# Decoder attention of a two-layer graph kernel: six pairs of weight tiles per block as seven half-size products

## The chip, the core and the metric

The kernel runs on one core of one Trainium2 chip. The metric is the device time of one launch in microseconds. The core has five engines with queues of their own: TensorE (PE in the profile, its weight loads PEld), VectorE (DVE), ScalarE (ACT), GpSimd (POOL) and SyncE (SP, which here only issues transfers). PE reads on-chip memory (SBUF) and writes eight accumulator banks (PSUM), each 128 partitions by 512 fp32 numbers.

## The reference, cut to what matters

Two graph layers on 4096 nodes with 512 features and a dense 0/1 adjacency `adj`. Layer 0 has an encoder attention, a block of products with batch norm, a decoder attention that uses the encoder's attention weights again, and a second such block. Layer 1 is a graph attention. Both of layer 0's masks are `adj`, so both of its softmaxes are the same. The change is in the line that makes `Y`:

```python
sig = jax.nn.sigmoid(f1[:, :, None] + f2[:, None, :])
att = masked_softmax(adj * sig, adj != 0)          # encoder and decoder, 4 heads
Xa  = jnp.einsum('hij,hjd->hid', att, Xw)          # encoder
...
Yh  = emb.reshape(n, H, D).transpose(1, 0, 2)
Y   = jnp.einsum('hij,hjd->hid', att, Yh)          # decoder
Y   = jnp.einsum('hnd,hed->hne', Y, W)
Yc  = jax.nn.elu(Y.transpose(1, 0, 2).reshape(n, F))
out = mlp_block(Yc, dec_mlp_W, dec_mlp_b, ...)
```

## The kernel before, in words

Everything is fp32 and feature-major: a tensor of one head is 128 features (partitions) by 4096 nodes. `attention` (L222) serves encoder, decoder and graph attention. It walks eight blocks: four heads `h` times two halves `tb` of the target nodes (TB = 2048 columns). In each block it walks 32 source tiles `j` of 128 nodes. For each it makes a weight tile `e` of 128 sources by 2048 targets, and PE multiplies it, in four products of 512 columns, with `block(values[h], j)`, a 128 by 128 piece of the head's values. The four products go to four PSUM banks `po`, each accumulated over the 32 tiles (L377). The fourth bank is taken only at tile `EVICT` = 2, when a bank of the block before has come free, and catches up the first two tiles there (L374).

In the decoder a weight tile is made by `tanh_weights` (L469): a tanh and an exponential on ACT (L471, L472), and a product with the mask tile on DVE (L473). Every fifth tile (j % 5 == 4, six of 32) was kept by the encoder in DRAM and is only read back (L347). Mask tiles are loaded on SP, five ahead at most (L211). The weight tiles come from six buffers in rotation: `weight_tile` (L253) takes two from a pool `keep` and, in the decoder, four from its own. The tile six further on can be started only when PE has finished with the one in its buffer.

The steps that end a block are not done at its end: `at(j, f)` puts them in a list, and they are issued at tile j of the next block. At `EVICT` the function `ending` (L298) copies the four banks out with `out_dec` (ACT, L708). The reciprocal denominators from the encoder are fetched by POOL (`spread`, L288, at tiles 11, 12, 18 and 19); six tiles later `scaled` (DVE, L587) multiplies a quarter with them, and one tile later `elu` (L711) does an exponential on ACT (L714) and two steps on DVE (L715, L716). `pinned` and `issue_after` only keep an instruction behind named ones of its own engine. The rest of the order in each engine's queue is made by the framework's scheduler when the kernel is built.

Before the decoder, `w` (128 by 2048, one of the large buffers) holds the encoder block's weights; the decoder block's weights are loaded into it (L719) ahead of the decoder. After the decoder, `mlp_block` (L631) starts with products of the first three heads for seven column ranges before it needs the last head.

The denominators of the encoder and of layer 1 are products with 32 columns of ones (L266), four of them side by side in one bank.

Of the kernel before, what the change touches and what calls it, by code (L numbers as in the profile page):

```python
# [31 lines left out]
FP = mybir.dt.float32  # L32
U8 = mybir.dt.uint8
AF = mybir.ActivationFunctionType
ALU = mybir.AluOpType
# [4 lines left out]
N, F, H, D, P = 4096, 512, 4, 128, 128  # L40
IB = 512
NIB = N // IB
NJ = N // P
C = IB // P

TB = 2048
NTB = N // TB
SB = TB // IB
# [26 lines left out]
EVICT = 2  # L75
INVERT = 4


VECS = [
    "enc_bn_gamma", "enc_bn_beta", "enc_mlp_b", "enc_mlp_bn_gamma", "enc_mlp_bn_beta",  # L80
# [5 lines left out]
def kernel(ctx, tc, x, xT, adjT, w0, w0T, v0, wencT, wdecT, vecs, w1, w1T, a1, outT):  # L86
    nc = tc.nc
    consts = ctx.enter_context(tc.tile_pool(name="consts", bufs=1))
# [9 lines left out]
    w = big.tile([P, C, F], FP, name="w")  # L98
# [4 lines left out]
    def block(r, j):  # L103
        return r[:, j * D:(j + 1) * D]

    def bank():
        return psum.tile([P, IB], FP, name="ps")

    def bank1():
        return psum1.tile([P, IB], FP, name="den")  # L110
# [21 lines left out]


    score = consts.tile([P, 2, NTB, H, NJ // NTB], FP, name="score")
    jcol = consts.tile([P, NTB, H, NJ // NTB], FP, name="jcol")
    jcol2 = consts.tile([P, NTB, H, NJ // NTB], FP, name="jcol2")
    nq = consts.tile([P, NTB, H, NJ // NTB], FP, name="nq")

    def column(t, j, h):
        j = j % (NJ // NTB), j // (NJ // NTB)  # L140
# [80 lines left out]

    def attention(what, keep, pools, weights, values, row_of, out, finish, ebufs, modes=None, invert=None,  # L222
                  kept=None, sums=None, sums2=None, extras={}, row0=None, masks0=(), in_parts0=1,
                  finish_last=None, behind=()):

# [20 lines left out]
        spool, made, masks0 = pools, 0, list(masks0)  # L248
# [45 lines left out]
        def at(j, f, *args):  # L294

            later.setdefault(j, []).append(lambda: f(*args))
# [20 lines left out]
        def next_row_of(h, tb):  # L317
            rowb = keep.tile([P, TB], FP, name="rowb", bufs=2)
            load_row(rowb, *row_of(h, tb))
            return rowb  # L320

        later, last_ones, last_main, products_of = {}, None, None, ()
        rowb = row0 if row0 is not None else next_row_of(0, 0)
        blocks = [(h, tb) for h in range(H) for tb in range(NTB)]
        for n, (h, tb) in enumerate(blocks):
            last = n == len(blocks) - 1
            moved, by_ones, *ends_later = modes(n) if modes is not None else ((), ())
            den = bank1() if invert is not None else None
            begun = False
            into = sums2[0 if n else 1] if moved else None  # L330

            po, ahead, late = [bank() for _ in range(SB - 1)], [], []
            adds, held, stores, at_end, next_row = [], [], [], [], None
            for j in range(NJ):

# [8 lines left out]
                e = weight_tile()  # L344
# [3 lines left out]
                else:  # L348
# [6 lines left out]
                    with pinned([*(products_of[:1] if kept == "read" and n == 0 and j < 8 else ()),  # L355
                                 *(behind if n == 0 and j < EP else ())]):
                        products_of = weights(e, rowb, a, j, h, SB if NJ * n + j < in_parts0 else 1)


                    if stores and (store if n > 1 else j % KEEP == KEEP - 3):  # L360
                        k, t = stores.pop()
                        (nc.sync if n > 1 else nc.scalar).dma_start(ekeep[h][tb][k], t)
                    if store:
                        stores.append((j // KEEP, e))

                def products():
                    nonlocal last_main, last_ones

                    with tc.issue_after(last_ones.ins) if last_ones is not None else nullcontext():

                        if j == EVICT:
                            po.append(bank())
                            for k, t in ahead:
                                nc.tensor.matmul(po[-1], block(values[h], k), t[:, (SB - 1) * IB:SB * IB],  # L374
                                                 start=(k == 0), stop=False)
                        for s, b in enumerate(po):
                            last_main = nc.tensor.matmul(b, block(values[h], j), e[:, s * IB:(s + 1) * IB],  # L377
                                                         start=(j == 0), stop=(j == NJ - 1))
                    last_ones = None
# [3 lines left out]
                    late.append((j, e))  # L383
                else:
                    products()
                if j < EVICT:
                    ahead.append((j, e))
                if invert is not None:
                    if j in moved:

# [33 lines left out]
                    at(EVICT, (nc.sync if n > 1 else nc.scalar).dma_start, ekeep[h][tb][k], t)  # L424
            if not last:

                at(EVICT, ending, h, tb, po, den if invert is not None else None,
                   4 if kept == "write" and n == 0 else 0)
                if ends_later:
                    at(1, add_to_den, den, into, False, True)  # L430
                rowb = next_row
                continue
            for s, b in enumerate(po):
                for k, t in late:
                    nc.tensor.matmul(b, block(values[h], k), t[:, s * IB:(s + 1) * IB], start=(k == 0),
                                     stop=(k == NJ - 1))
# [41 lines left out]
    with tc.tile_pool(name="keep", bufs=1) as keep:  # L478

        with tc.tile_pool(name="f_small", bufs=1) as small, tc.tile_pool(name="f_work", bufs=2) as work:  # L480
# [5 lines left out]
            for ib in range(NIB):  # L486
# [7 lines left out]
                for c in range(0, C, 1 if ib == 0 else C):  # L494
                    n = 1 if ib == 0 else C
                    load = nc.sync.dma_start(xs[ib][:, c:c + n, :], xin[:, c:c + n, :])
# [10 lines left out]
            for ib in range(NIB):  # L507
# [45 lines left out]
                for c in range(C):  # L553
                    j = ib * C + c
# [150 lines left out]

        def out_dec(spool, h, tb, s, po):
            o = nodes(xd[h], tb * SB + s)
            nc.scalar.copy(o, po)  # L708
            return o

        def elu(spool, h, tb, s, o, rb, last):  # L711

# [3 lines left out]
            nc.vector.scalar_tensor_tensor(o, o, 0.0, ex, ALU.max, ALU.add)  # L716


        nc.sync.dma_start(w, wdecT.rearrange("(c p) o -> p c o", p=P))  # L719
        with tc.tile_pool(name="dec", bufs=1) as spool:  # L720
            attention("dec", keep, spool, tanh_weights, xc, lambda h, tb: (rows[tb], h), out_dec, (scaled, elu), 4,
                      kept="read", behind=behind_it)


    v1 = xd

    edge = ctx.enter_context(tc.tile_pool(name="edge", bufs=1))
    with tc.tile_pool(name="l_small", bufs=1) as small, tc.tile_pool(name="l_work", bufs=2) as work:
        x1 = [R[2]] + [small.tile([P, N], FP, name=f"x1_{o}") for o in range(1, C)]

# [275 lines left out]
```

## Time and profile before

| | us |
|---|---|
| median of three runs (3239.97 to 3241.52) | 3239.99 |
| the profiled execution, its own time | 3242.24 |
| its span, first to last instruction | 3240.5 |
| PE busy in the span | 3187.6 (98%) |
| DVE busy | 2665.8 (82%) |
| ACT busy | 2581.8 (80%) |
| POOL busy | 477.6 (15%) |
| products of L377, 6008 instructions | 2608.1 |

The span is a row of stages: layer norm and first products up to about 69 us, the encoder attention to 1039, its block of products to 1184, the decoder attention to 2065, its block of products and the second layer norm to about 2315, and the graph attention to the end. The mean granted TensorE clock is 0.996 of full speed. An fp32 product appears as two instructions. The mean duration of one matmul instruction (595 ns in L377) is longer than the distance from one to the next (0.429 us), because they are pipelined; time is read from the distances. A group line of the profile has line, engine, operation, output and inputs with shapes and count, then busy time and mean duration in ns, then the idle time of the engine just before, with what ended it.

### The profile page before, as it was taken

How to read it: one execution, taken by the hardware profiler on the slowest of the kernel's cores; microseconds unless marked ns; L12 is line 12 of the kernel's file. 1: busy time of each engine (PE TensorE's matmuls, PEld its weight loads, DVE VectorE, ACT ScalarE, POOL GpSimd, SP SyncE). 2: the span in 40 equal slices, each digit the busy share in tenths (PEclk: the TensorE clock that was granted, in tenths of full speed). 3: DMA queues.
4: the chain of work that ended last, by engine and by line, in shares of the span. 5: the costliest groups of instructions: out<-in, count | busy, mean ns of one | idle time of the engine just before them, and what ended most of it. 6: DMA issues, size and time to landing. Idle time of an engine off the chain costs nothing.

```text
span 3240.5 us, 25992 instructions
## 1 busy us (share of the span) xinstructions
PE 3187.6 (98%) x8675; PEld 1477.3 (46%) x8675; DVE 2665.8 (82%) x1945; ACT 2581.8 (80%) x1825; POOL 477.6 (15%) x624
## 2 busy tenths in 40 slices
PE   7999999999999999999999999999999999999998
PEld 6334444444444464444444444448644444444443
DVE  7989999999999665655665665585699999999998
ACT  7999999999997459999999999566765665665663
POOL 3001211211210000000000000025412222122221
PEclk9999999999999999999999999999999999999999
DMA  9998988988986024443443443231489999899996
GB/s 210 198 198 242 273 223 231 268 222 229 268 236 159 7 69 141 143 143 126 139 153 130 133 145 133 62 123 63 130 201 221 214 229 237 218 213 235 229 215 156
DMA packets 212023, 580.60 MB, mean 179 GB/s; under 512 B 25168, under 2 KB 28272, under 8 KB 195888
## 3 DMA queue, kind: packets, MB, share of 16 engines
q0 software_dynamic: 68256, 223.56, 36.5%
q1 hardware_dynamic: 132200, 332.53, 30.1%
q10 hardware_dynamic: 11432, 22.85, 2.0%
q8 instruction: 68, 1.11, 0.1%
q14 instruction: 67, 0.55, 0.0%
HBM read 378.15 MB, written 84.30 MB: 143 GB/s over the span
## 4 chain that ended last, share of the span: by engine, by line
PE 50%; DVE 24%; issue 13%; DMA 9%; ACT 3%; DVEq 0%; POOL 0%; SPq 0%; ACTq 0%; POOLq 0%
PE ps L377 35%; DVE e L923 7%; DVE R L402 7%; PE ps L639 7%; DVE e L473 4%; DMA a<-mask 4%; DMA w<-e 4%; DVE acc L402 4%; PE ps L828 3%; DMA acc<-e 2%; ACT e L471 1%; PE den L266 1%; ACT e L472 1%; PE ps L699 1%; PE ps L374 1%
## 5 line engine op out<-in xcount | busy, mean ns | idle before, releaser
L377 PE MATMUL ps<-e,R 128*128 128x512 f32 x6008 | 2608.1, 595 | 25.0 <-DVE e L473 20.6
L377 PEld LDWEIGHTS ps<-e,R 128*128 128x128 f32 x6008 | 1137.8, 190 | 1489.6 <-issue 1394.3
L473 DVE TENSOR_TENSOR e<-e,a 128x2048 f32<-128x2048 f32 (+1 forms) x470 | 1053.2, 2261 | 388.1 <-ACT e L472 365.0
L471 ACT ACTIVATE e<-rowb,score 128x2048 f32<-128x2048 f32 (+1 forms) x470 | 911.8, 1968 | 78.7 <-PE ps L377 43.4
L472 ACT ACTIVATE e<-e 128x2048 f32<-128x2048 f32 (+1 forms) x470 | 869.3, 1879 | 7.9 <-DVE e L473 2.6
L922 ACT ACTIVATE e<-rowb,nq,jcol 128x2048 f32<-128x2048 f32 x224 | 459.4, 2088 | 265.6 <-DMA w<-e 141.2
L923 DVE SCALAR_TENSOR_TENSOR e<-e,jcol,a 128x2048 f32<-128x2048 f32 (+1 forms) x265 | 591.2, 2260 | 2.8 <-ACT e L922 2.8
L402 DVE TENSOR_TENSOR R<-R,e 128x2048 f32<-128x2048 f32 x128 | 291.1, 2274 | 0.0
L402 DVE TENSOR_TENSOR acc<-acc,e 128x2048 f32<-128x2048 f32 x121 | 276.4, 2285 | 0.9
L392 POOL DMA_DIRECT2D w<-e x178 | 149.4, 845 | 610.8 <-DMA w<-e 294.6
L639 PE MATMUL ps<-R,w 128*128 128x512 f32 x512 | 220.3, 592 | 0.6 <-DVE w L597 0.6
L392 POOL DMA_DIRECT2D acc<-e x146 | 122.5, 888 | 521.0 <-DMA acc<-e 233.4
L291 POOL DMA_DIRECT2D rb<-rinvs x60 | 33.9, 569 | 1054.8 <-DVE R L587 867.2
L639 PEld LDWEIGHTS ps<-R,w 128*128 128x128 f32 x512 | 97.2, 190 | 122.7 <-issue 117.7
L828 PE MATMUL ps<-w1x,hT 128*128 128x260 f32 x512 | 115.5, 384 | 1.4 <-ACT hT L806 1.4
L828 PEld LDWEIGHTS ps<-w1x,hT 128*128 128x128 f32 x512 | 96.5, 190 | 19.8 <-issue 3.3
L922 ACT ACTIVATE e<-w,nq,jcol 128x2048 f32<-128x2048 f32 (+1 forms) x41 | 67.4, 1708 | 25.5 <-DMA R<-e 25.4
L865 POOL TENSOR_TENSOR vacc<-vacc,R 128x128 f32<-128x128 f32 x120 | 65.8, 577 | 45.3 <-ACT R L858 44.9
L662 DVE SCALAR_TENSOR_TENSOR ex<-ex,re 128x512 f32<-128x512 f32 x64 | 44.9, 702 | 32.8 <-ACT re L661 32.6
L660 ACT ACTIVATE ex<-ps,bias 128x512 f32<-128x512 f32 x32 | 22.0, 689 | 58.8 <-PE ps L639 56.4
L858 ACT ACTIVATE R<-ps,rstd 128x128 f32<-128x128 f32 x128 | 38.5, 371 | 29.3 <-PE ps L828 25.6
L266 PE MATMUL den<-e,ones 128*32 128x512 f32 x416 | 51.7, 608 | 3.9 <-DVE e L923 3.9
(175 smaller groups left out, 1255.9 us busy)
## 6 DMA issues: line engine op xcount, KB each, us to landing
a<-mask SPq DMA_DIRECT2D x720, 256.0 KB, 4.1
w<-e POOLq DMA_DIRECT2D x178, 512.0 KB, 6.9
acc<-e POOLq DMA_DIRECT2D x146, 512.0 KB, 6.9
e<-ekeep SPq DMA_DIRECT2D x48, 1024.0 KB, 4.9
ekeep<-e SPq DMA_DIRECT2D x36, 1024.0 KB, 6.9
mask<-in_adjT POOLq DMA_DIRECT2D x8, 2048.0 KB, 105.4
rowb<-rows SPq DMA_DIRECT2D x16, 1024.0 KB, 5.9
rb<-rinvs POOLq DMA_DIRECT2D x60, 256.0 KB, 4.6
```

Source lines behind the costliest of these rows:

```text
L266: last_ones = nc.tensor.matmul(den[s * 32:(s + 1) * 32, :], ones[:, 0:32], t[:, s * IB:(s + 1) * IB], start=start, stop=stop)
L377: last_main = nc.tensor.matmul(b, block(values[h], j), e[:, s * IB:(s + 1) * IB], start=(j == 0), stop=(j == NJ - 1))
L392: nc.gpsimd.dma_start(into_half, e_half, **({"accum_op": ALU.add} if j > moved[0] else {}))
L402: nc.vector.tensor_add(acc, acc, e)
L471: nc.scalar.activation(e, rowb, AF.Tanh, bias=column(score[:, 1], j, h), scale=0.5)
L472: last_act = nc.scalar.activation(e, e, AF.Exp, scale=0.5)
L473: last_dve = nc.vector.tensor_mul(e, e, a)
L639: last = nc.tensor.matmul(z, w[:, fb, o * P:(o + 1) * P], nodes(src[fb], ib), start=(fb == 0), stop=(fb == C - 1))
L828: m = nc.tensor.matmul(banks[k][:, 0:2 * DX], hT[:, fb, c * P:(c + 1) * P], w1x[:, fb, 2 * k:2 * k + 2, :].rearrange("p h x -> p (h x)"), ...
L865: nc.gpsimd.tensor_add(vacc[:, h, :], vacc[:, h, :], block(v1[h], j))
L922: last_act = nc.scalar.activation(e, rowb, AF.Relu, bias=column(nq, j, h), scale=column(jcol, j, h))
L923: last_dve = nc.vector.scalar_tensor_tensor(e, e, column(jcol2, j, h), a, ALU.add, ALU.mult)
```

## The change

In the decoder alone, the 128 value features are cut in two halves of 64, and the 2048 targets in two halves of 1024. Two source tiles `j` and `j+1` then make a 2 by 2 by 2 product of blocks, which needs eight block products, and in Strassen's form seven. This is done for six pairs in each block: tiles (5, 6), (8, 9), (11, 12), (14, 15), (17, 18) and (20, 21). The other 20 tiles are multiplied as before, but each product of 128 columns as two of 64 (`halves`), whose outputs lie in partitions 0 to 63 and 64 to 127 of a bank.

The sums of value blocks are made once a head by `stationaries` (three steps on POOL, one on DVE) into `z`, which lies in `w`; so the load of the next block's weights into `w` moves to tile 24 of the last block. The sums of weight tiles are made in each pair on DVE (`sums_first`, `sums_second`), one of them in place. Four more banks (`aux`) take up products that serve more than one output; all eight banks are held through the decoder, and `po` and `aux` change places from block to block. Six tiles after the last pair, `aux_out` copies the four auxiliary banks out on ACT, and POOL copies their halves across partitions; at tile 1 of the next block `combined` adds on DVE; at tile 3 `out_dec`, now on DVE, adds or subtracts the result while it evicts the banks. The fourth quarter is swapped between partition halves by two more copies. Three small tiles (`jcol`, `jcol2`, `nq`) move to a pool that is opened later.

```diff
+HB = TB // 2
+HD = D // 2
+PAIRS, STEP, FIRST = 6, 3, 5
...
+        pairs = [FIRST + STEP * k for k in range(PAIRS)] if fast is not None else []
+        banks8 = [*(bank() for _ in range(7)), bank1()] if fast is not None else []
+
+        def halves(b, g, weight, x, start, stop):
+            return nc.tensor.matmul(b[g * HD:(g + 1) * HD, :], weight, x, start=start, stop=stop)
+
+        def sums_first(e):
+            t = [spool.tile([P, HB], FP, name=f"t{k}", tag=f"t{k}", bufs=2) for k in range(3)]
+            nc.vector.tensor_add(t[0], e[:, 0:HB], e[:, HB:TB])
+            return t
+
+        def sums_second(t, e1, e2):
+            nc.vector.tensor_add(t[1], t[0], e2[:, HB:TB])
+            nc.vector.tensor_add(e1[:, HB:TB], e1[:, HB:TB], e2[:, HB:TB])
+            return nc.vector.tensor_add(t[2], t[1], e2[:, 0:HB])
+
+        def seven(k, v, po, aux, t, e1, e2):
...
+            into(po[2], 0, z[3], e2[:, HB:TB], 0, False)
+            into(po[3], 1, z[3], e2[:, HB:TB], 1, False)
+            for part in range(2):
+                into(aux[part], 0, one[:, 0:HD], e1[:, 0:HB], part, True)
+                into(aux[part], 1, z[1], t[1], part, True)
+            for part in range(2):
+                into(aux[2 + part], 0, z[0], t[0], part, True)
+                into(aux[2 + part], 1, z[2], e1[:, HB:TB], part, True)
+            for part in range(2):
+                into(po[part], 0, two[:, 0:HD], e2[:, 0:HB], part, False)
+                made = into(po[part], 1, two[:, HD:D], t[2], part, False)
+            return made
+
+        def aux_out(h, tb, aux, m):
+
+            o = block_of(fast[1][h], tb)
+            for s, b in enumerate(aux):
+                nc.scalar.copy(o[:, s * IB:(s + 1) * IB], b)
+            m.extend(spool.tile([P, HB], FP, name=f"t{k}", tag=f"t{k}", bufs=2) for k in range(2))
+            for k in range(2):
+                for g in range(2):
+                    nc.gpsimd.dma_start(m[k][g * HD:(g + 1) * HD, :],
+                                        o[(1 - g) * HD:(2 - g) * HD, k * HB:(k + 1) * HB])
...
+        def combined(h, tb, m):
+
+            o = block_of(fast[1][h], tb)
+            lo, hi = slice(0, HD), slice(HD, P)
+            nc.vector.tensor_add(m[0], m[0], o[:, 0:HB])
+            nc.vector.tensor_add(o[hi, 0:HB], m[0][hi, :], o[hi, HB:TB])
+            nc.vector.tensor_add(m[0][hi, 0:IB], m[0][hi, 0:IB], m[1][hi, 0:IB])
+            nc.vector.tensor_add(m[0][lo, IB:HB], m[0][lo, IB:HB], o[lo, HB + IB:TB])
+            nc.vector.tensor_add(o[:, HB:HB + IB], o[:, HB:HB + IB], m[0][:, 0:IB])
+            nc.vector.tensor_add(o[:, HB + IB:TB], m[1][:, IB:HB], m[0][:, IB:HB])
...
+                if j in pairs:
+                    e1, sums_of = e, sums_first(e)
+                elif j - 1 in pairs:
+                    made_sums = sums_second(sums_of, e1, e)
+                    products_of = products_of[0], made_sums
...
+                    if fast is not None:
+                        if j - 1 in pairs:
+                            last_main = seven(pairs.index(j - 1), values[h], po, aux, sums_of, e1, e)
+                        elif j not in pairs:
+                            for s, b in enumerate(po):
+                                for g in range(2):
+                                    f = (g + s // (SB - 1)) % 2
+                                    last_main = halves(b, g, block(values[h], j)[:, f * HD:(f + 1) * HD],
+                                                       e[:, s * IB:(s + 1) * IB], j == 0, j == NJ - 1)
+                        return
...
+                if fast is not None and j == pairs[-1] + 1:
+                    m = []
+                    at(j + 6, aux_out, h, tb, aux, m)
+                    at(1 if not last else NJ - 1, combined, h, tb, m)
...
-                at(EVICT, ending, h, tb, po, den if invert is not None else None,
+                at(EVICT if fast is None else 3, ending, h, tb, po, den if invert is not None else None,
...
             o = nodes(xd[h], tb * SB + s)
-            nc.scalar.copy(o, po)
+            if s < SB - 1:
+                (nc.vector.tensor_add if s < 2 else nc.vector.tensor_sub)(o, po, o)
+                return o
+            turned = spool.tile([P, IB], FP, name="exd", bufs=2)
+            nc.vector.tensor_sub(turned, po, o)
+            for g in range(2):
+                nc.gpsimd.dma_start(o[g * HD:(g + 1) * HD, :], turned[(1 - g) * HD:(2 - g) * HD, :])
             return o
+
+        z = w.rearrange("p c f -> p (c f)")[:, 0:4 * PAIRS * HD].rearrange("p (i k c) -> p i k c", i=4, c=HD)
+
+        def stationaries(h):
+            v = xc[h][:, FIRST * D:(FIRST + STEP * PAIRS) * D].rearrange("p (k c) -> p k c", c=STEP * D)
+            a11, a21, a12, a22 = (v[:, :, i * HD:(i + 1) * HD] for i in range(4))
+            nc.gpsimd.tensor_sub(z[:, 0], a22, a21)
+            nc.gpsimd.tensor_sub(z[:, 2], a11, a21)
+            nc.vector.scalar_tensor_tensor(z[:, 1], z[:, 0], -1.0, a11, ALU.mult, ALU.subtract)
+            nc.gpsimd.tensor_add(z[:, 3], a12, z[:, 1])
...
-        nc.sync.dma_start(w, wdecT.rearrange("(c p) o -> p c o", p=P))
+                      kept="read", behind=behind_it, fast=(z, xd, stationaries),
+                      extras={(H * NTB - 1, 24): decoder_weights})
```

## The prediction

> **What bounds the kernel now.** I read the 40 slices first (TensorE, PE, is at 9 almost throughout), then the chain of waits, to learn who sets the end in the decoder, which is the only stage that the change touches:
>
> ```profile
> 1412.59 108.15 PE ps L377 x252
> 1522.46 108.15 PE ps L377 x252
> ```
>
> Columns: start, length, what. From block to block it is 109.87 us, all of it PE: 32 tiles x 4 products x 2 instructions = 256 instructions of 0.429 us. A product of 128x128 by 128x512 thus takes 0.858 us, a tile 3.43. The stretch 1200 to 2065 holds eight such blocks without a gap worth naming. Then a table of busy time over one block-long stretch (PE, weight loads, DVE, ACT, POOL):
>
> ```profile
> 1410.00:1520.00 110.00, 110.00 (x258) 48.70 (x257) 65.94 (x38) 103.04 (x61) 2.15 (x4) 1.00 0.42 139
> ```
>
> PE is full, but ACT is busy for 103 of 110: whatever PE gives up, ACT can follow for some 6 us a block and no more. DVE has 44 us free. The prices come from the groups by form and from stretches of the timeline:
>
> ```profile
> L473 DVE TENSOR_TENSOR e<-e,a 128x2048 f32<-128x2048 f32 x462 | 1047.8, 2288 | 387.2 <-ACT e L472 364.1 <-DMA a<-mask 12.2 <-PE ps L377 10.8
> L587 DVE TENSOR_TENSOR R<-R,rb 128x512 f32<-128x512 f32 x60 | 40.5, 684 | 13.0 <-ACT R L708 12.1 <-DMA rb<-rinvs 0.9
> L810 DVE TENSOR_TENSOR sq<-sq 128x1024 f32<-128x1024 f32 x8 | 9.8, 1225 | 15.9 <-ACT sq L805 13.3 <-ACT sq L809 2.7
> ...
> 1488.72 4.49 DVE L473 TENSOR_TENSOR e<-e,a 128x2048 f32<-128x2048 f32 x2 [3.29 <-ACT e L472]
> ...
> 1426.84 1.99 ACT L471 ACTIVATE e<-rowb,score 128x2048 f32<-128x2048 f32 x1
> 1428.86 1.91 ACT L472 ACTIVATE e<-e 128x2048 f32<-128x2048 f32 x1
> 1430.67 1.99 ACT L471 ACTIVATE e<-rowb,score 128x2048 f32<-128x2048 f32 x1
> ```
>
> Two masks back to back take 4.49, so each costs 2.21 of DVE's time, 0.08 less than its 2.29; I take the same 0.08 off the others: 1.14 for a 128x1024 sum, 0.60 for 128x512. A tile costs ACT 3.84 (tanh to tanh). Last, what half-width products cost. The kernel has products of 32 columns (the denominators):
>
> ```profile
> 439.87 1.92 PE L266 MATMUL den<-e,ones 128*32 128x512 f32 x16
> 441.62 1.90 PE L266 MATMUL den<-acc,ones 128*32 128x512 f32 x16
> 443.44 5.42 PE L377 MATMUL ps<-e,R 128*128 128x512 f32 x12
> ```
>
> Thirty-two instructions last 3.57 us from 439.87 to 443.44, against 13.7 if they ran one by one at 0.429: four at a time, each group of columns on its own moving data, with 0.14 lost at the change of width.
>
> **What the Trainium skill says.** "TensorEngine Tiling (Array Packing)", Key Properties: column tiles of 64 make two independent tiles, and a change of mode drains the array. The denominators agree on both counts, for 32 columns; no row shows 64. "TensorE: Matmul & The Clock Gate", What overlaps and what doesn't (Part 3): products complete in program order. So a product that waits holds everything behind it. "VectorE: DVE Perf Modes", errata section: an fp32 tensor_tensor takes (N+151)/0.96 ns, 1224 ns at N=1024; L810 measures 1225. "TensorE", Architectural detail: ScalarE and VectorE queues are strictly first in, first out, which matters to the slower rival below.
>
> **The change, part by part.**
>
> *PE.* A pair had 8 full products; it has 7 slots of two halves. Per block 20 x 4 + 6 x 7 = 122 slots in place of 128: 122 x 0.858 = 104.7 us, 5.15 less, 41.2 over eight blocks. Every other product is split in two halves beside each other and should keep its 0.858. Bounds: no loss, as in the denominators, or, if halves don't overlap at all, double. I take no loss; two changes of width cost 0.2 each. The fourth bank now starts with the others, so L374 goes; its work was the same.
>
> *DVE, per block.* Masks 26 x 2.21 = 57.5 (six tiles of 32 are read from DRAM). Sums for pairs: 6 x 4 x 1.14 = 27.4, and about 0.1 more where one reads the result of the one just before (L716 starts 0.46 after the L715 that it reads, others 0.34 after): 1.2. `combined`: 2 x 1.14 + 4 x 0.60 + 0.3 = 5.0. `out_dec`, now on DVE: 4 x 0.61 = 2.4. `scaled` and `elu` as before: 4 x (0.60 + 0.35 + 0.72) = 6.7. One product for `stationaries` every other block, 0.2 on average. Sum 100.4.
>
> *ACT, per block.* 26 x 3.84 = 99.8, four copies 2.0 (of the auxiliary banks now, of the outputs before), four exponentials of `elu` at 0.52: 103.9. Unchanged, and only 0.8 below PE's new 104.7.
>
> *POOL and SP.* Four copies within SBUF at tile 27, needed by `combined` at tile 1 of the next block, some 20 us later; accumulating transfers of comparable size land in 6.9, so they are hidden. Three 128x384 sums for each head, at most 1.6 each (the 128x512 ones of L744 take 1.56), beside ten tiles of PE. The load of `w` moves behind the last pair of the last block: SP waits there, and mask tiles 25 and on wait behind it on SP, 4.1 to land plus 2.2 for the mask; PE has tiles 22 to 24 (10.3 us) meanwhile. If that cover fails it costs a few us once.
>
> *Where it doesn't run side by side.* Between tiles 5 and 21 the DVE has more to do than PE, so I add both up from PE's start of a block at t=0. Before, DVE ended tile 3's mask 1.4 after it (1404.88+2.29 against 1405.72); with `combined` ahead of tile 1 it is a good tile later, so I let it end tile 2's mask at 1.8. Until tile 18's mask is done it then has: outputs 2.4, thirteen masks 28.7, four pairs complete 4 x 4 x 1.14 + 0.7 = 18.9, first sum of the fifth 1.2, two `scaled` and one `elu` 2.3: t = 55.3. PE reaches that pair at 5 x 3.43 + 4 x (6.01+3.43) = 54.9. A seven can begin on its last mask alone, but its second slot needs the sum t1 (1.24 later, covered by a slot of 0.86), so PE loses 0.4 + 0.2 of signalling and then 0.4. For pair (20, 21) DVE adds 3.5 + 1.1 + 2.2 + 1.2 + 2.2 = 10.2 and PE 6.0 + 3.4 plus those losses, again 0.8. So 1.8 a block, 106.5. Afterwards DVE has 11 tiles of slack to recover, and ACT, with six weight tiles in rotation, may idle 106.5 - 103.9 = 2.6. I take 107.0, half a us more for an order on ACT and DVE that isn't the best one: that order is the scheduler's, as the trace of before shows (the `scaled` of one quarter between the two DVE steps of another's `elu`), and it was not made for these queues.
>
> *Edges.* After the last block the DVE evicts and one output quarter takes a further copy; some 5 us more than now, beside the 21 first products of the MLP (18 us), which don't need that head.
>
> **Sum.** 8 x (107.0 - 109.87) = -23.0, +0.4 for changes of width: -22.6. The profiled execution took 3242.24 (span 3240.5), so 3219.6; the median of the runs is 2.25 below that execution: 3217.4.
>
> **Rivals.**
> 1. *Everything hides*: blocks of 104.7. The DVE's sums would have to be ahead when PE gets to the fifth and sixth pair. For it: 44 us free in DVE. Against: the walk above. 3240 - 41 = 3199.
> 2. *DVE dearer than priced*: every sum 1.22, without overlap (the form's full duration): 24 x 0.08 = 1.9 more a block, blocks near 108.5 to 110: 3229 to 3241.
> 3. *ACT waits for the DVE (slower).* The exponential of `elu` stands in ACT's queue. Before, it came directly behind a tile's exponential (it starts at 1451.62), harmless because DVE had done `scaled` at 1450.8. Now `scaled` of the first quarter stands behind a pair's sums: done at t = 48, when ACT has reached that place at 44.6; 3.4 to 4.3 lost. For the third quarter DVE passes tile 23 at 73.6, ACT at 65.7; after what was already lost some 5 remain; under 1 each for the other two. Together 10: ACT 103.9 + 10 = 114, +4.1 a block, 3240 + 33 = 3273. It decides from 6 us a block on (103.9 + 6 = 109.9). For it: ACT has nearly no slack, and the old order was just this one. Against: the order is made anew, and the step may go behind another tile.
> 4. *Halves run one after the other*: PE 209 a block, 3242 + 796, about 4040. Against: the denominators.
>
> **How the numbers follow.** Forecast 0.42 (3205 to 3228), rival 1 0.15, rival 2 0.15, rival 3 0.24, rival 4 0.04. A difference of 0.2% (6.5 us) is what a measurement of this kernel can tell from none. Faster 0.42 + 0.15 + half of rival 2 = 0.65; same 0.07, the rest of rival 2; slower 0.28. The range from 3197 to 3262 takes in rival 1's end and the milder part of rival 3, and leaves out some 0.18. The likeliest case alone: 3205 to 3228.
>
> **What would show it.** Blocks of about 107 us on PE, with short idle before L377's successors only in the fifth and sixth pair, ended by DVE sums; half products starting two per 0.429 us; DVE busy near 100 and ACT near 104 a block; the MLP's products directly behind the last block. Wrong if ACT idles before L714's exponential for several us a block (rival 3), if PE idles in every pair, or if the half products' spacing isn't half.

## The result, and the profile after

On the chip the changed kernel takes 3239.9 us (median of 12 runs, 3238.47 to 3240.93), the kernel before, run beside it, 3241.52 (12 runs). Two of those 12 (3348.9 and 3720.18) ran in a slower state of the chip, so the ratio is taken from the other runs alone. It is 0.9995, with a 95% interval of 0.9986 to 1.0004: no difference. The forecast was 3217.

The profiled execution took 3239.95 (span 3238.2). I measure the decoder from its first product to the first product of the next stage: 880.68 us before, 879.24 after. So TensorE's gain is either not there or given back inside the decoder. The table of busy time (stretch, its length, then busy us of PE, weight loads, DVE, ACT, POOL) for the first, the second and the fourth block of the kernel after:

```profile
1183.24:1299.37 116.13, 113.92 (x489) 43.78 (x489) 91.20 (x57) 107.16 (x61) 3.76 (x7) 1.00 0.43 139
1299.37:1407.68 108.31, 107.43 (x491) 43.43 (x489) 99.74 (x72) 101.71 (x61) 13.94 (x13) 1.00 0.47 152
1516.65:1625.62 108.97, 107.64 (x490) 39.52 (x488) 101.22 (x74) 102.02 (x61) 13.96 (x13) 1.00 0.47 152
```

A block before had 110 of 110 on PE and 66 on DVE. Now the first block is longer than before (116.13), the others 108.3 to 109.9, and DVE has 101. A block's 488 matmul instructions follow each other every 0.2146 us where nothing waits, 104.72 in all; the busy column shows up to 113.92 for the same instructions, so I go by the distances between them. What is above 104.72 is therefore waiting: 11.41 us in the first block (before: 1.74), 3.58 in the second, 4.25 in each of the six others (the last one loses about 1 more at its end). The sum is 40.5, nearly all of the 41.2 that PE was spared.

What ends the waits? The table of waits, blocks 2 to 7 (engine, what it wrote, line, what it waited for; us in total, times, longest):

```profile
DVE e L564 <- ACT e L563: 43.9, 26, 3.3
...
ACT e L562 <- PE ps L327: 17.9, 17, 2.6
PEld ps L327 <- DVE t L335: 16.6, 23, 1.4
PEld ps L327 <- DVE e L564: 15.3, 18, 1.5
...
ACT exd L824 <- DVE R L678: 3.3, 6, 0.6
```

PE waits for DVE, for the second sum of a pair (L335) and for masks (L564). ACT waits for PE to free a weight tile's buffer, DVE waits for ACT. Each engine of the three waits for the next one, and none is full. The chain of waits in one block (start, length, what) shows where it turns:

```profile
by line: DVE e L564 27.7%; issue 18.5%; ACT e L562 10.5%; PE ps L327 9.0%; ACT e L563 6.8%; DVE t L331 5.6%; DVE t L335 5.3%; DVE t L337 4.5%; ACT R L366 1.7%; DVE t L382 1.3%; DVE t L383 1.3%; DVE R L800 1.2%; DVE R L381 1.1%; DVE t L380 1
...
1581.35 4.40 DVE e L564 x2
1585.75 1.15 DVE t L335
...
1586.95 3.66 PE ps L327 x15
...
1592.55 1.99 ACT e L562
...
1620.17 1.22 DVE t L380
```

Before, the chain was PE alone. Now PE has 9% of it. DVE carries it through the pairs; then the sixth pair's products free a buffer, ACT carries it through the last third of the block, and DVE takes over at `combined` (L380). The stretch of DVE's timeline in front of the sixth pair:

```profile
1577.33 2.29 DVE L564 TENSOR_TENSOR e<-e,a 128x2048 f32<-128x2048 f32 x1
1579.53 0.69 DVE L826 SCALAR_TENSOR_TENSOR R<-R,exd 128x512 f32<-128x512 f32 x1
1580.13 1.22 DVE L331 TENSOR_TENSOR t<-e 128x1024 f32<-128x1024 f32 x1
1581.27 4.49 DVE L564 TENSOR_TENSOR e<-e,a 128x2048 f32<-128x2048 f32 x2
1585.67 1.22 DVE L335 TENSOR_TENSOR t<-t,e 128x1024 f32<-128x1024 f32 x1
```

No row has an idle time in brackets: DVE has work without a rest, from `combined`, 5.5 us ahead of the block's start, for some 84 us. And two masks stand between the first sum of the pair (20, 21) and its second, L335: tile 21's, which it needs, and tile 22's, which it doesn't. PE waits 1.67 us there, in each of these blocks. The other waits of such a block are 0.77 in the pair (11, 12), where again the next mask stands ahead of the second sum, and 1.25 ahead of and 0.52 in the pair (17, 18), where none does.

### The profile page after: what moved, and what is told of

It reads as the page before. It is cut to its first block, busy times and chain, and to the rows that moved or that the text cites. A ratio compares the mean times of both kernels' runs of the same rounds, so it can differ in the third digit from the quotient of the medians.

```text
span 3238.2 us, 30083 instructions
## 1 busy us (share of the span) xinstructions
PE 3174.8 (98%) x10531; PEld 1412.9 (44%) x10531; DVE 2939.0 (91%) x2221; ACT 2577.6 (80%) x1825; POOL 532.8 (16%) x684
## 4 chain that ended last, share of the span: by engine, by line
DVE 34%; PE 23%; issue 18%; ACT 15%; DMA 8%; DVEq 0%; POOL 0%; ACTq 0%; SPq 0%; POOLq 0%
DVE e L564 9%; ACT e L562 9%; DVE e L1036 8%; DVE R L493 7%; PE ps L730 7%; PE ps L327 6%; ACT e L563 5%; PE ps L941 3%; DMA a<-mask 3%; PE ps L464 3%; DMA w<-e 2%; DMA acc<-e 2%; DVE acc L493 2%; DVE t L331 1%; DVE t L335 1%
## 5 line engine op out<-in xcount | busy, mean ns | idle before, releaser
L464 PE MATMUL ps<-e,R 128*128 128x512 f32 x3992 | 1738.8, 595 | 24.7 <-DVE e L564 20.4
L464 PEld LDWEIGHTS ps<-e,R 128*128 128x128 f32 x3992 | 754.4, 190 | 1005.3 <-issue 923.8
L564 DVE TENSOR_TENSOR e<-e,a 128x2048 f32<-128x2048 f32 (+1 forms) x470 | 1053.0, 2269 | 124.7 <-ACT e L563 105.4
L327 PE MATMUL ps<-e,R 128*64 128x512 f32 x2624 | 758.6, 593 | 1.6 <-DVE e L564 1.5
L1036 DVE SCALAR_TENSOR_TENSOR e<-e,jcol,a 128x2048 f32<-128x2048 f32 (+1 forms) x265 | 610.5, 2385 | 2.8 <-ACT e L1035 2.8
L327 PEld LDWEIGHTS ps<-e,R 128*64 128x64 f32 x2624 | 246.8, 136 | 315.2 <-issue 312.9
L493 DVE TENSOR_TENSOR R<-R,e 128x2048 f32<-128x2048 f32 x128 | 308.2, 2408 | 0.0
L327 PE MATMUL den<-e,R 128*64 128x512 f32 x320 | 159.9, 592 | 0.0
L327 PE MATMUL ps<-e,w 128*64 128x512 f32 x288 | 134.3, 596 | 4.3 <-DVE e L564 4.3
L327 PE MATMUL ps<-t,w 128*64 128x512 f32 x336 | 108.8, 597 | 5.2 <-DVE t L335 4.5
L327 PE MATMUL ps<-t,R 128*64 128x512 f32 x192 | 90.2, 592 | 0.0
## 6 DMA issues: line engine op xcount, KB each, us to landing
mask<-in_adjT POOLq DMA_DIRECT2D x8, 2048.0 KB, 106.5
```

The source lines that it names most:

```text
L327: return nc.tensor.matmul(b[g * HD:(g + 1) * HD, :], weight, x, start=start, stop=stop)
L493: nc.vector.tensor_add(acc, acc, e)
L564: last_dve = nc.vector.tensor_mul(e, e, a)
L1036: last_dve = nc.vector.scalar_tensor_tensor(e, e, column(jcol2, j, h), a, ALU.add, ALU.mult)
```

## The experiments

Theories. *Order*: the waits come from masks that the scheduler put ahead of a pair's sums. *Amount*: they come from DVE's added work itself. *ACT and buffers*: ACT, without slack, is what holds the block. *Density*: pairs every third tile are more than DVE can do in PE's time, and the lead that six buffers allow doesn't last over six pairs; *buffers*: a longer lead would. From the forecast stand its rivals 3 (ACT waits for DVE ahead of `elu`'s exponential) and 4 (halves don't run beside each other). All edits below are made to the kernel after, if not said otherwise. The lengths in this table are worked out from the traces, as distances between first products; each ratio is to the kernel before as it ran beside that version:

| run | decoder | first block | a later block | kernel, median | ratio to before, 95% interval |
|---|---|---|---|---|---|
| before | 880.68 | 111.6 | 109.87 | 3241.52 | |
| after | 879.24 | 116.13 | 108.97 | 3239.9 | 0.9995 (0.9986 to 1.0004) |
| e1 sums first | 871.75 | 115.06 | 106.8 to 109.9 | 3232.68 | 0.9973 (0.9964 to 0.9982) |
| e2 combined at 31 | 875.11 | 116.11 | 108.29 | 3235.52 | 0.9985 (0.9978 to 0.9991) |
| e3 no sums | 841.28 | 107.66 | 104.72 | 3201.98 | 0.988 (0.9867 to 0.9894) |
| e4 halves only | 880.63 | 111.46 | 109.87 | 3241.06 | 1.0003 (0.9994 to 1.0011) |
| e5 every fourth tile | 855.50 | 110.56 | 106.33 | 3217.55 | 0.9928 (0.9915 to 0.994) |
| e6 e5 and e1 | 855.28 | 110.02 | 106.33 | 3214.23 | 0.9919 (0.9905 to 0.9933) |
| e7 first sum on POOL | 927.49 | 118.53 | 116.02 | 3288.08 | 1.0146 (1.0132 to 1.016) |
| e8 seven buffers | 855.93 | 113.84 | 105.88 | 3217.71 | 0.9927 (0.9914 to 0.9939) |
| e9 e5, e1 and e8 | 842.12 | 108.15 | 104.72 | 3202.35 | 0.9883 (0.9869 to 0.9897) |
| e10 first block plain | 875.70 | 113.53 | 108.95 | 3235.57 | 0.9985 (0.9978 to 0.9991) |
| e11 e8 and e1 | 857.91 | 112.25 | 106.39 | 3216.95 | 0.9929 (0.9915 to 0.9943) |
| e12 e9 and early table | 840.86 | 106.90 | 104.72 | 3202.23 | 0.988 (0.9862 to 0.9897) |

**Is the gain there at all?** Two runs take the change apart. e4 has no pairs: all 32 tiles as half products, outputs copied as before.

```diff
-        pairs = [FIRST + STEP * k for k in range(PAIRS)] if fast is not None else []
+        pairs = []
...
-                                    f = (g + s // (SB - 1)) % 2
+                                    f = g
```

> No pairs: all 32 tiles are multiplied as half products, the outputs are copied out by ACT at tile 2 as in the kernel before, no sums, no combined. It tells the price of half products, of eight held banks and of the later load of w. If halves are as cheap as the trace of the changed kernel shows (0.2146 us each): blocks 109.87, 3236 to 3242. If the first block's 11.4 us of stalls came from anything but the pairs, they show here too: 3246 or more.

e3 keeps the seven products and leaves out the 24 sums of weight tiles a block; parts of the weight tiles stand in their places, so DVE's additions are not in its time.

```diff
-            nc.vector.tensor_add(t[0], e[:, 0:HB], e[:, HB:TB])
-            return t
+            return [e[:, 0:HB], e[:, HB:TB], e[:, 0:HB]]
...
-            nc.vector.tensor_add(t[1], t[0], e2[:, HB:TB])
-            nc.vector.tensor_add(e1[:, HB:TB], e1[:, HB:TB], e2[:, HB:TB])
-            return nc.vector.tensor_add(t[2], t[1], e2[:, 0:HB])
+            return products_of[1]
```

> The four sums of weight tiles per pair are left out; the seven products take slices of the two weight tiles in their place. 24 DVE steps, 27 us a block, go. Theories 'amount' and 'order': PE runs its 122 slots without a stall, 104.7 a block, and the first block loses under 4 us in place of 11: 3197 to 3206. Theory 'ACT and buffers' (ACT needs 103.9 of 104.7): blocks stay at 107 or above, 3220 or more.

A block of e4, then one of e3, in the table of busy time:

```profile
1514.74:1624.61 109.87, 109.87 (x516) 36.78 (x514) 66.13 (x39) 103.36 (x61) 2.15 (x4) 1.00 0.42 139
```

```profile
1500.00:1604.72 104.72, 104.72 (x490) 42.82 (x488) 71.88 (x46) 100.47 (x61) 10.32 (x13) 1.00 0.51 159
```

In e4 the 512 instructions of 256 half products take the time of the 256 instructions of 128 full ones. In e3 PE is full again, at 104.72. So halves cost nothing (rival 4 falls), the 5.15 us a block are real, and the decoder gets 39.4 shorter as soon as DVE's sums are gone, with every other part of the change in place: four output additions, `combined`, the copies on ACT and POOL. Without the sums the whole gain is there.

**Is it their order?** e1 holds the mask of the tile after a pair behind the pair's last sum.

```diff
                                  *([made_sums] if j - 2 in pairs else ()),
```

> The masks of the two tiles after a pair may no longer stand ahead of that pair's sums on DVE. Theory 'order' (masks 13 and 22 put ahead of sums hold back the sevens of pairs (11,12) and (20,21)): those two stalls, 0.77 and 1.67 us a block, go; blocks 108.97 to 106.5 or so, the whole about 20 us less than the changed kernel's 3239.9, near 3220. Theory 'amount' (DVE has work for 89 us of a block without a rest, whatever its order): the stall only moves to another pair or mask; at most 4 us less, 3236 to 3241. Theory 'ACT and buffers': no change, 3238 to 3242.

From the second block on, nearly all of the waits in the pairs (11, 12) and (20, 21) is gone, as order had it. But 2.1 to 5.1 us a block are now lost, nearly all at tile 16 and in the pair (17, 18), though no mask that the pair doesn't need stands ahead of its second sum there, and ACT's wait for `scaled` grew from 3.3 to 17.2 us over six blocks (rival 3's wait, which the change itself doesn't have). Of the 41 us this brings 7.5, net of the new wait. So with six buffers and pairs at every third tile, a better order alone is not enough.

e2 makes `combined` in its own block's last tile and not at tile 1 of the next.

```diff
-                    at(1 if not last else NJ - 1, combined, h, tb, m)
+                    at(NJ - 1, combined, h, tb, m)
```

> The six sums of combined (about 6 us of DVE with their waits) are issued at tile 31 of their own block in place of tile 1 of the next. Theory 'amount': they fall into the gaps in which DVE waits for ACT (7 us a block between tiles 27 and 0), so the stretch without rest starts 5 us earlier against PE; PE's stalls fall from 4.26 to 1 or less a block; 20 to 26 us less, 3214 to 3220. Theory 'order': the same masks stand ahead of the same sums, stalls stay above 2.5; at most 10 us less. Theory 'ACT and buffers': no change.

Only the wait of 0.77 shrinks, to 0.09: 0.68 a block. Five microseconds of DVE's work taken out of the busy stretch bring next to nothing: in the time they leave, DVE now rests 0.7 us ahead of the block's start and 1.1 us some 27 us into it, until ACT has made the next weights.

**Is it density, or the lead?** e5 has a pair at every fourth tile (5, 9, ... 25). In the last block its sixth pair is multiplied with what the next stage's load has then put into `w`, so these products have other numbers, in the same time. e6 adds e1's edit.

```diff
-PAIRS, STEP, FIRST = 6, 3, 5
+PAIRS, STEP, FIRST = 6, 4, 5
...
-                    at(j + 6, aux_out, h, tb, aux, m)
+                    at(j + 4, aux_out, h, tb, aux, m)
```

> The same six pairs a block, but every fourth tile: (5,6), (9,10), (13,14), (17,18), (21,22), (25,26); the auxiliary banks leave at tile 30. All amounts as in the changed kernel. Theory 'density' (in the stretch of pairs DVE needs 3 x 2.21 + 4 x 1.14 = 11.2 a pair and its neighbour, PE only 9.4; with one more tile between it is 13.4 against 12.9): stalls fall from 4.25 to under 1.5 a block and in the first block from 11.4 to 7 or less; 3208 to 3218. Theory 'amount' (the sum of DVE's work in a block, 100, is too near to PE's 104.7): stalls stay at 3 to 5 a block, 3232 to 3242.

> As e5, and masks may not stand ahead of a pair's sums (e1's edit). Theory 'density': the order matters little where DVE keeps up, within 5 us of e5. Theory 'order' as the larger part: 8 us or more below e5, as e1 was below the changed kernel.

e8 gives the weight tiles a seventh buffer, and takes one of `t2` for its room.

```diff
-            t = [spool.tile([P, HB], FP, name=f"t{k}", tag=f"t{k}", bufs=2) for k in range(3)]
+            t = [spool.tile([P, HB], FP, name=f"t{k}", tag=f"t{k}", bufs=2 - k // 2) for k in range(3)]
...
-            attention("dec", keep, spool, tanh_weights, xc, lambda h, tb: (rows[tb], h), out_dec, (scaled, elu), 4,
+            attention("dec", keep, spool, tanh_weights, xc, lambda h, tb: (rows[tb], h), out_dec, (scaled, elu), 5,
```

> A seventh weight tile in rotation (the third sum has one buffer in place of two). Nothing else moves. Theory 'buffers' (DVE's lead at tile 10 is cut short because tanh of tile 11 waits for a buffer, 1.4 us in e2): DVE and ACT enter the pairs one tile (3.4 us) further ahead; stalls 4.25 to 1 or less a block, 3208 to 3218. Theory 'density' alone: DVE is late by 1.9 us a pair however much lead it has at the start; six pairs use up 11 us; at most half of the stall goes: 3222 to 3232.

Both, each alone, bring the decoder down by 23 to 24 us, though neither takes a single instruction off DVE. e8 shows why. DVE's timeline ahead of the pair (17, 18), its two masks, in the kernel after and in e8:

```profile
1566.38 2.29 DVE L564 TENSOR_TENSOR e<-e,a 128x2048 f32<-128x2048 f32 x1
...
1571.25 2.30 DVE L564 TENSOR_TENSOR e<-e,a 128x2048 f32<-128x2048 f32 x1
```

```profile
1556.63 2.29 DVE L564 TENSOR_TENSOR e<-e,a 128x2048 f32<-128x2048 f32 x1
...
1561.51 4.49 DVE L564 TENSOR_TENSOR e<-e,a 128x2048 f32<-128x2048 f32 x2
```

The blocks start at 1516.65 and 1510.29. In the kernel after, tile 18's mask ends at 1573.55, 56.9 into the block. In e8 I take it as the first of the two, which ends at about 1563.8, 53.5 into the block; PE is there at 54.9 at the earliest, and its first product there does not wait. Already tile 2's mask is done at 0.66 in place of 4.19: the further buffer makes everything 3.5 us earlier, the time of one plain tile on PE. How far DVE may be ahead is set by the number of buffers, and this lead, and not only DVE's sum of work, decides whether six pairs in a row can be fed.

What is left in e8 is 1.16 a block, in the last two pairs. In e5 all that is left is 1.6 in the pair (17, 18), and e6 doesn't change it: its decoder is 0.2 shorter, so the 3.3 us between the two medians don't come from there (in the profiled executions 1.5 of them lie ahead of the decoder). But e6 does not clear the order of blame for this wait. DVE's timeline there, in e6:

```profile
1558.66 4.49 DVE L565 TENSOR_TENSOR e<-e,a 128x2048 f32<-128x2048 f32 x2
1563.06 1.22 DVE L335 TENSOR_TENSOR t<-t,e 128x1024 f32<-128x1024 f32 x1
```

Two masks stand ahead of the second sum, and the pair needs only the first, tile 18's. e1's edit holds back the mask of the one tile right behind a pair; here that is tile 19, which is read from DRAM and has none, so the next mask slips in, as in e5. It takes 2.2 us, more than the 1.6 that PE waits for the sum. In e8, both pairs that still wait have such a mask too (the fence above shows one of them).

e7 takes a sum off DVE:

```diff
-            nc.vector.tensor_add(t[0], e[:, 0:HB], e[:, HB:TB])
+            nc.gpsimd.tensor_add(t[0], e[:, 0:HB], e[:, HB:TB])
```

> Pairs as in the changed kernel, but the first of a pair's four sums is made by POOL. DVE has 6 x 1.14 = 6.8 us less in a block, and per pair and neighbour 10.1 in place of 11.2. POOL takes about 3 us for it (twice its 1.6 for 128x512), beside the mask of the next tile. Theory 'density': stalls fall by more than half, to 2 or less a block: 3218 to 3226. If POOL's sum comes too late for the second sum, PE stalls at every pair and the time is 3245 or more.

It lost 48 us. Groups by form of e7, five blocks (count, busy us, mean ns of one, idle before and what ended it):

```profile
L331 POOL TENSOR_TENSOR t<-e 128x1024 f32<-128x1024 f32 x30 | 110.1, 3669 | 138.4 <-DVE e L564 132.7 <-DMA e<-ekeep 5.7
...
L336 DVE TENSOR_TENSOR e<-e 128x1024 f32<-128x1024 f32 x30 | 45.3, 1510 | 0.0
...
L335 DVE TENSOR_TENSOR t<-t,e 128x1024 f32<-128x1024 f32 x30 | 36.8, 1225 | 47.4 <-POOL t L331 46.4
```

POOL needs 3.67 us for the sum that DVE makes in 1.22, DVE waits some 9 us a block for it, and one of DVE's own sums, L336, rises from 1.22 to 1.51. The Trainium skill names a possible reason in "SBUF — State Buffer", section Who interferes with whom: the two engines share a pair of ports under an exclusive lock, and a VectorE instruction with two SBUF inputs contends with a GpSimd instruction that reads SBUF. These rows agree with it, but no run has POOL's sum alone.

**The first block.** It loses 11.41 us and saves 5.15. e10 leaves the pairs out of it, as the kernel before had it, with half products.

```diff
+            pairs = all_pairs if n else []
...
-                                    f = (g + s // (SB - 1)) % 2
+                                    f = (g + s // (SB - 1)) % 2 if n else g
...
+            if h == 0 and tb == 0:
+                nc.scalar.copy(o, po)
+                return o
```

> The changed kernel, whose first decoder block has no pairs: eight products there, at full size, and its four results are copied by ACT. Theory: the first block starts with an empty queue of exponentials, DVE and ACT have no lead there, and the pairs' sums put 11.4 us of waits into it, to save 5.15 us of products. Without pairs it takes the 111.5 us that it took before the change, in place of 116.1, and the next block starts with a fuller queue and less of DVE's work owed (its own combination of results is gone): 3233 to 3236 us. Rival: the first block's loss is that of the four stationaries made at its start and of what stands behind them; then it stays at 115 or more, and the time at 3239 or above.

Its waits fall to 3.65, so the pairs make 7.8 of the 11.4. But the block took 113.53, 2 us more than expected. Of the 3.65, 1.6 stand at tile 7, where the kernel before waits too (1.5); the rest is new, at tiles 2 and 3. ACT's timeline at the decoder's start shows what is new there; first of the kernel before, then of the kernel after:

```profile
1161.18 0.20 ACT L172 ACTIVATE coefs<-coefs 128x1 f32<-128x1 f32 x1 [3.80 <-DVE coefs L171]
1161.40 1.28 ACT L471 ACT_TABLE_LOAD   x1
1184.28 2.00 ACT L471 ACTIVATE e<-rowb,score 128x2048 f32<-128x2048 f32 x1 [21.60 <-PE ps L699]
```

```profile
1160.23 0.20 ACT L173 ACTIVATE coefs<-coefs 128x1 f32<-128x1 f32 x1 [3.80 <-DVE coefs L172]
1184.12 1.28 ACT L562 ACT_TABLE_LOAD   x1 [23.68 <-DVE R L791]
1185.41 2.00 ACT L562 ACTIVATE e<-rowb,score 128x2048 f32<-128x2048 f32 x1
```

Loading ACT's table for tanh takes 1.28 us in both (the Trainium skill, "ScalarE: Activation LUTs", section What ACT_TABLE_LOAD costs, has 1283 ns; the further 1380 ns of draining that it states aren't seen here: the tanh begins 1.29 us after the load does). Before, the load lay in ACT's idle time. After, it stands behind a wait for DVE's last step of the stage before, and the first weights made in this stage come later. No edit of the change asks for this.

**Together.** e11 has e8's and e1's edits, e9 also pairs at every fourth tile, and the load into `w` at tile 28, after the last pair.

> Pairs at every third tile as in the changed kernel, with the sums kept ahead of the next mask and seven buffers (t2 has one). If the place of the sums and the number of buffers are the two causes of the waits, and density counts only through them, the blocks come to 105 to 105.5 us and the first to 112 to 113.5: 3210 to 3215 us. If density counts by itself (five sums' worth of DVE work for each three tiles is more than TensorE's time for them), the waits at the fifth and sixth pair stay, blocks at 105.9 as with the buffers alone: 3217 us.

> Pairs at every fourth tile (5, 9, ... 25), the sums of a pair kept ahead of the next mask, seven buffers for the exponentials (t2 then has one), and the load of the next weights after the last pair. Theory 'density and buffers': these parts act on the same queue, DVE's, so their gains (8.1, 23.7, 23.5 us alone) do not add up; they are bounded by TensorE's own 104.7 us a block. I expect blocks 1 to 7 at 104.8 to 105.6 us and the first block at 108 to 110, so 3204 to 3211 us. Rival: the wait of 1.6 us at tile 17 in the runs with every fourth tile isn't one for a buffer, then the blocks stay at 106.3 and the time at about 3214. Rival: with two of the three sums' buffers doubled only, the one t2 makes pairs wait for each other, then 3217 or more.

At every third tile, holding the sums ahead adds nothing to the seventh buffer (the decoder even gets 2 us longer): 1.66 us a block stay in the pair (20, 21). That would speak for density by itself, but the order is not right there. DVE's timeline in front of that pair, in e11:

```profile
1569.36 1.22 DVE L331 TENSOR_TENSOR t<-e 128x1024 f32<-128x1024 f32 x1
1570.50 4.48 DVE L565 TENSOR_TENSOR e<-e,a 128x2048 f32<-128x2048 f32 x2
1574.90 1.22 DVE L335 TENSOR_TENSOR t<-t,e 128x1024 f32<-128x1024 f32 x1
```

Again two masks stand ahead of the second sum. The edit keeps tile 22's mask back, so after tile 21's the scheduler put that of a later tile, tile 23 by the order of ACT's exponentials. It costs that sum 2.2 us, and PE waits 1.66 for it. In e9 no pair has such a mask ahead of its second sum. So e9 and e11 differ in the density and in the order together, and which of the two takes the last 1.66 us away is not shown; an e11 with all later masks held back would tell.

In e9 the waits inside a block are gone in every block but the first. Busy time of its first and fourth block, then the head of the chain of waits in the fourth:

```profile
1183.10:1291.25 108.15, 106.56 (x490) 46.17 (x490) 91.11 (x57) 107.12 (x61) 3.75 (x7) 1.00 0.49 158
1500.68:1605.40 104.72, 104.72 (x491) 49.09 (x489) 100.91 (x74) 101.84 (x61) 12.11 (x13) 1.00 0.47 158
```

```profile
by line: PE ps L327 80.8%; PE den L327 19.3%
```

DVE and ACT have the same 101 and 102 us of work as in the kernel after. PE alone sets the end, as before the change, and the decoder takes 842.12, 0.8 more than without any sums. The kernel is faster than both, 0.9883 of the one before. Which of its three edits it could do without wasn't tried.

e12 adds to e9 a tanh of one column, right after the last coefficients.

```diff
+            warm = small.tile([P, 1], FP, name="warm")
+            nc.scalar.activation(warm, b_mlp[:, C - 1:C], AF.Tanh)
             for h in range(H):
                 w2 = work.tile([P, D], FP, name="w2", bufs=2)
```

> The version with every fourth tile, sums first and seven buffers, and one more instruction: a tanh of one column on ACT right after the last coefficients, so that ACT's table of tanh is loaded there and not at the decoder's first tile. In the traces of all versions with pairs, the 1.28 us load begins at the decoder's start, after the wait for the VectorE step that ends the stage before; in the kernel before it stood 22 us earlier, in ACT's idle time, and the first block's first weights came 1.1 us sooner and 2 us sooner against PE's start. Theory 'table load': the first block loses 1.67 and 0.31 us at its second and third tile through it; with the early load the first tanh starts at most 0.2 us after that VectorE step, the block comes to 106.5 to 107.0 in place of 108.15, the kernel to 3200.5 to 3201.5 us. Rival: the first weights are late for the VectorE step, not for the load; then the block stays within 0.3 of 108.15 and the time at 3202.

```profile
1162.23 1.28 ACT L780 ACT_TABLE_LOAD   x1
1166.06 0.20 ACT L780 ACTIVATE warm<-coefs 128x1 f32<-128x1 f32 x1 [2.55 <-DVE coefs L185]
1185.90 2.01 ACT L563 ACTIVATE e<-rowb,score 128x2048 f32<-128x2048 f32 x1 [19.63 <-DVE R L794]
```

The load went to ACT's idle time, and the first block is 106.90, 1.25 shorter, as expected. The kernel's time is not: 3202.23 against e9's 3202.35, and in this execution the decoder began 1.9 us later. A gain of 1.25 can't be told in the whole kernel's time here; it is shown for the block alone.

## Why the prediction was wrong, by its own steps

*PE.* Right. 104.7 a block, 5.15 less, no loss through halves: e4 and e3 show both.

*DVE and ACT, per block.* Right in size. DVE 100.4 forecast, 99.7 to 101.2 measured; sums follow each other at 1.14, as taken. ACT 103.9 forecast, 102.0 measured. So rival 2 (dearer sums) is refuted as a mechanism, though the time lies at its end.

*POOL and SP.* The load of `w` and the copies across partitions hold up nothing that the waits show. A sum of `stationaries` was costed at 1.6 at most and took up to 6.57, still hidden.

*Where it doesn't run side by side.* This is the step that failed, in its term "So 1.8 a block, 106.5" and the half us on it: 4.25 a block were measured. Place and releaser were right in the main: PE waits in the pairs (17, 18) and (20, 21), for DVE. The size was not. The walk let DVE end tile 2's mask at 1.8 and tile 18's at 55.3; measured are 4.19 and 56.9. It took DVE's start from the trace of before and added `combined`, as if DVE could otherwise run ahead; but the weight tiles' buffers allow no more lead, and what ACT and DVE lose in the pairs isn't made up by "11 tiles of slack": the exponential of a block's tile 0 ended 12.2 us ahead of the block's start before the change, 7.7 after it, still 7.7 in e2, and 11.2 in e8 with its seventh buffer. The sixth pair costs 1.67 in place of 0.8, the fifth 1.77 in place of 1.0, and 0.77 in the third, (11, 12), was not forecast: in the third and the sixth the scheduler set the next mask ahead of the sum. The blocks take 108.97 in place of 107.0.

*Edges.* Failed too. The first block was costed like the others: 107.0 in place of 116.13. It begins with only two finished weight tiles, and its waits were not looked for (before the change it took 111.61, which the sum put at 109.87). It alone is 9.1 of the some 21 us between forecast and result. e10 gives 7.8 of its waits to the pairs, and e12, measured on e9, 1.25 to the table load.

*Sum.* Forecast: 41.2 off PE, 18.2 given back in waits and 0.4 in changes of width, -22.6. Measured: 41.2 off PE, 38.8 more waits than before, and about 1 at the last block's end, -1.4.

*Rivals.* The third, ACT behind `scaled`, is not in the kernel after: that wait is 0.6 us a block. It appears in e1 (17.2 us over six blocks), so its mechanism exists and hangs on the order. The first, everything hides, is what e9 reaches, at 3202.35, with three further edits, to the lead, the density and the order.

## What to carry to other kernels

Free time on an engine, 44 us of 110 here, doesn't say that added work hides: ask how densely it comes where it comes, what else stands in the queue ahead of it, and how far the engine may run ahead, which the number of buffers in rotation limits. When three engines are each above 95% of the new bound, look for the version in which the added work is spread out and one more buffer is in rotation, before shortening anything; here the two, with the sums held ahead of the next mask, gave no engine more work, and brought 38.6 of the 41.2 us. After an edit that holds one instruction behind another, read the new order from the trace: the scheduler may put a third in the gap. Cost the first pass of a pipeline apart, because it starts with little lead, and look in it for one-off work, such as a table load, that a new wait pushes onto the path.

## What the hardware showed that I had not expected

Half products of 64 columns, two beside each other in fp32, run at the full rate without any loss: their 512 instructions take 109.87 us a block (e4), as the 256 of full products did.

POOL and DVE hold each other up for more than one instruction. The first step of `stationaries` on POOL in the kernel after, and the third, of the same size, a little later:

```profile
1371.12 6.57 POOL L813 TENSOR_TENSOR w<-R 128x384 f32<-128x384 f32 x1 [16.88 <-PE ps L327]
...
1383.08 0.99 POOL L816 TENSOR_TENSOR w<-R,w 128x384 f32<-128x384 f32 x1 [0.36 <-DVE w L815]
```

A step of one size takes 6.57 us and 0.99, and so it is in three of the four heads, those whose steps lie beside the decoder's products. While the first ran, DVE went through four steps with two SBUF inputs each without a rest, up to 1376.82, and POOL's step ended at 1377.69. Then it was DVE's turn to lose: its next two steps took 1.98 us beside the end of POOL's first step and its second, where one takes 0.43 in the median, and the mask beside POOL's third took 3.02 in place of 2.29. By these rows a short step on POOL can wait through a chain of DVE's instructions, and it lengthens those that it then overlaps.
